# Perceiver stack on one core: the prologue reordered and one context normalised on three engines, and the last chunk's convolution, logarithm and final group rewritten

## The chip, the cores and the metric

The kernel runs on 1 core of one Trainium2 chip, as one launch. The metric is the device time of that launch in microseconds, the median of three runs. The engines are TensorE (PE, with its weight loads PEld), VectorE (DVE), ScalarE (ACT), GpSimd (POOL), and SyncE (SP), whose queue issues nearly all DMAs.

## The reference, cut to what matters

Sixteen batches of 64 latent rows of 128 features (`x`) attend to 1601 context rows per batch, twice, with a scan and a feed-forward after each attention. All is float32.

```python
x = x + xattn0(ctx, ln(x))         # 16 heads of 64; keys/values: 1601 context rows + 64 latents
x = x + selective_scan(ln(x))      # layer 0 "attn"
x = x + moe(ln(x))                 # layer 0 "ffn", 8 experts, top 2
x = x + xattn1(ctx, ln(x), mask)   # layer 1, masked
x = x + ssd(ln(x))                 # layer 1 "attn"
x = x + fp4_ffn(ln(x))             # layer 1 "ffn", blockwise FP4 quantised

# ssd, per batch of 64 tokens, 256 inner channels, 4 heads:
x, z = split(h @ in_proj.T)
x = silu(conv1d_causal(x, conv_w, width=4) + conv_b)
dt = softplus(x @ dt_w.T + dt_b)   # 4 values per token
h  = exp(A * dt) * h + dt * B * x ; y = C . h + D * x
out = (ln(y) * silu(z)) @ out_proj.T
```

## The kernel before

**Staging.** Attention is cut into 64 groups, each a layer, a batch and half of the heads. A group has `NT = 13` steps: step i takes 128 keys against 512 columns (8 heads by 64 latents). The global step number is n, from 0 to 832 for the scores. `step(n)` issues the scores of tile n, and the weighted average (`average`) of the tile `LAG = 21` steps behind. Scores land in PSUM (tag `s`, 3 buffers), ACT copies them to SBUF (`st`, line 625 with mask, 627 without), DVE keeps a running maximum (`R`, lines 632 and 634). `maximum`, `spread` and `weigh` turn them into exponentials (DVE line 669, ACT line 670), and `average` adds 13 products into one PSUM tile `av` (line 682), of which there is one buffer. `gather` (line 693) reads it, `denominator` divides, `turn` transposes, `output` multiplies by the folded output weights `wvo` and adds to the residual `X`. For the last group a few extra matmuls without use (`fill`) are placed on PE in the waits.

**What runs between.** `run` holds two lists. `prep` holds generators that prepare contexts, queries and latents, each with the step n from which it may run; each live one is advanced by one `yield` per step, and a yielded tuple such as `HOP3 = (3,)` makes it sit out three steps. `between` holds the scans and feed-forwards, advanced within a budget per step (0.65 to 1.0 a step, capped at 2.0), in which a yielded number is the cost that is charged. `behind` keeps what it encloses from being issued ahead of the attention instructions of its step, and a scheduler then fixes each engine's static order. In layer 1 the last stages are `scan1` and `ffn` for chunk 6 and chunk 7 (128 tokens each). Chunk 6 may run from n = 810, chunk 7 only when the last group's result is in `X`: it is the tail after the attention. After n = 853 what is left of all stages is issued interleaved.

**Prologue.** `setup` issues the first loads and warms PE with 12 `fill` matmuls. It then advances the generators `latents`, `fold_qk`, `queries` and `first_context` in an order written out by hand, and `in_order` freezes that order for each engine. `first_context` normalises batch 0's context in blocks of four tiles: statistics on DVE (`bn_stats`), the power −1/2 on POOL, the scaling on DVE, ACT or POOL. `context` does it for every later batch: the mean by two DVE reductions (line 571), the variance by 13 ACT squares with an accumulated sum (line 577), the power on POOL (line 129), POOL's offset (line 583), 13 ACT scalings (line 586), a store to DRAM, PE transposes (line 594) and ACT copies into `kvT` (line 595). Scores of batch 1 begin at n = 26. `with_latents` scales `kv` on POOL (line 556). The loads of context 2 (`context_load`) are issued at n = 8.

**The tail.** `scan1` for one chunk: layer norm (`moments`: DVE statistics, POOL multiply-add, POOL power), transpose to `hT`, projection `xz` (line 1055), ACT copy to the padded `xp`, the convolution as 8 DVE operations (lines 1066 and 1068), tanh (1071), then `dt` with a softplus (abs, exp, add, ACT `Ln` at line 1107, corrections), decays `af` (1119, 1151, 1154), `gm` (1161), `sy` (1167), layer norm, gate, `project`. `ffn`: layer norm, `quant` (line 1205 on), two projections (1262, 1263), silu, `quant` of 22 blocks, four transposes (1277), one ACT copy (1279), eight matmul records (1285), the addition and the store. PSUM tiles of these stages come from `tp`, 3 buffers.

Of the kernel before, what the change touches and what calls it, by code (L numbers as in the profile page):

```python
# [70 lines left out]

CG = 2
# [5 lines left out]
class Kernel:  # L78
# [35 lines left out]

    def fill(self, n, after=None):


        t = self.pss.tile([P, NQ], F32, tag="s", name="fill")
        free = mybir.DependencyInfo(mybir.DependencyClass.NoSync, mybir.DependencyReason.DATA)
        for _ in range(n):  # L120
            if after is None:
                mm = self.nc.tensor.matmul(t[:, :P], self.ident, self.ident, start=True, stop=True)
            else:
                mm = self.nc.tensor.matmul(t[:, :2 * P], self.ident, self.wvo[:, :2, :].rearrange("p h d -> p (h d)"), start=True, stop=True)
                self.tc.add_manual_dep(mm.ins, after.ins.name, free, reason="fill")
# [5 lines left out]
    def moments(self, src, n, outs, square=False):  # L131
# [14 lines left out]
        for a, b in outs:  # L146
            v, r = self.sm([P, n], f"var{n}"), self.sm([P, n], f"rstd{n}", bufs=4)
            nc.gpsimd.tensor_scalar(v, var, a, b, ALU.mult, ALU.add)
            self.rsqrt(r, v, n)
            rs.append(r)  # L150
# [6 lines left out]
    def layernorm(self, dst, src, n):  # L157

        mv, (r,) = self.moments(src, n, [LN])
# [5 lines left out]
    def transpose_tokens(self, dst, src, n, name, w=None, b=None):  # L165
# [5 lines left out]
        if w is None:  # L171
            nc.scalar.copy(dst, t[:, :n * P])
# [30 lines left out]
    def setup(self):  # L203
# [3 lines left out]
        self.fill(12)  # L207
# [4 lines left out]
        nc.sync.dma_start(out=self.X[:, :CG], in_=xs[:, :CG])  # L212
        self.raw0 = [self.raw_pair(0, "WqT", "WkT", 0, nc.scalar)]
        rows = self.at.tile([12, D], F32, tag="vrow", name="vrow")
        nc.scalar.dma_start(out=rows, in_=a["vec128"].rearrange("(n d) -> n d", d=D))
# [21 lines left out]
        nc.vector.tensor_scalar_mul(self.nvcol, t[:, :12], -1.0)  # L237

        for g in (context, fold, fold, latents, latents, context, context, queries, queries, context, queries):
            next(g)  # L240
        self.in_order()
# [238 lines left out]
    def first_context(self):  # L480
# [6 lines left out]
        mv = self.sm([P, n, 2], "fmv", bufs=1)  # L487
# [21 lines left out]
        def turned(lo, hi):  # L509
# [4 lines left out]
            nc.scalar.activation(kvT[:, lo * P:lo * P + w], t[:, :w], AF.Copy, scale=self.vcol[:, w1:w1 + 1])  # L514
# [7 lines left out]
        yield 0.0  # L522
# [39 lines left out]
    def context(self, lay, b):  # L562
# [5 lines left out]
        if lay == 0:  # L568
# [16 lines left out]
            for k in range(n):  # L585
                nc.scalar.activation(kv[:, k, :D], kv[:, k, :D], AF.Identity, scale=rstd[:, k:k + 1], bias=off[:, k:k + 1])  # L586
                if k % 5 == 4:
                    yield 0.0
            nc.sync.dma_start(out=self.xh[b], in_=kv[:, :, :D])
# [82 lines left out]
    def average(self, g, i):  # L672
# [6 lines left out]
        for k in range(4):  # L679
            o = grp["av"][:, k // 2, k % 2 * (D + 1):(k % 2 + 1) * (D + 1)]  # L680
            st = grp["st"][i // 2][:, i % 2, k * P:(k + 1) * P]
            mm = nc.tensor.matmul(o, st, self.kv_of[lay, b][0][:, i, :], start=(i == 0 and k % 2 == 0), stop=(i == NT - 1 and k % 2 == 1))  # L682
        if (g, i) == (len(self.groups) - 1, NT - 1):
            self.fill(3, mm)
# [11 lines left out]

    def denominator(self, g):
# [3 lines left out]

        eng = nc.vector if g == len(self.groups) - 1 else nc.gpsimd
        eng.tensor_tensor(aq[:, :, :D], aq[:, :, :D], self.bc(rd, [P, 4, D]), ALU.mult)  # L703
# [327 lines left out]

    def scan1(self, c0, CG):
# [5 lines left out]
        with tc.tile_pool(name="sd1", bufs=1) as one, tc.tile_pool(name="sd2", bufs=CG) as work:  # L1038
# [6 lines left out]
            xi, hT = t1([P, CG, D], "xi"), t1([P, TG], "hT")  # L1045
            xp = t1([P, 2, BG, L + 3], "xp")
            nc.gpsimd.memset(xp, 0.0)
            yield from self.layernorm(xi, X, CG)
# [4 lines left out]
            t = self.tp("xz")  # L1053
            for k in range(2):
                mm = nc.tensor.matmul(t[:, k * TG:(k + 1) * TG], inT[:, k * P:(k + 1) * P], hT, start=True, stop=True)
            if last:
                self.fill(9, mm)
            nc.scalar.copy(xp[:, :, :, 3:], t[:, :2 * TG].rearrange("p (k b l) -> p k b l", k=2, l=L))
            yield 0.5
            yield HOP1  # L1060

            cv = self.tp("cv")
            for k in range(2):
                o = cv[:, k * TG:(k + 1) * TG].rearrange("p (b l) -> p b l", l=L)
                cw = lambda i: self.half[:, 4 * k + i:4 * k + i + 1]
                nc.vector.tensor_scalar(o, xp[:, k, :, 0:L], cw(0), self.half[:, 8 + k:9 + k], ALU.mult, ALU.add)
                for i in range(1, 4):
                    nc.vector.scalar_tensor_tensor(o, xp[:, k, :, i:i + L], cw(i), o, ALU.mult, ALU.add)
                yield 1.6
# [12 lines left out]
            e, w, ln = (t1(shape, n) for n in ("spe", "spw", "spl"))  # L1082
# [12 lines left out]
            nc.vector.tensor_scalar_add(w, e, 1.0)  # L1095
            nc.vector.scalar_tensor_tensor(fl(z), fl(zb), 1.0, t[:, :2 * TG], ALU.add, ALU.mult)
            yield 0.8
# [9 lines left out]
            nc.scalar.activation(ln, w, AF.Ln)  # L1107
            nc.vector.scalar_tensor_tensor(w, w, 1.0, e, ALU.subtract, ALU.subtract)
# [3 lines left out]
            nc.vector.tensor_tensor(ln, ln, w, ALU.subtract)  # L1112
            nc.vector.scalar_tensor_tensor(dt, dt, 0.0, ln, ALU.max, ALU.add)
            nc.vector.tensor_tensor(adt, dt, self.row(self.na1, shape), ALU.mult)

            full = [P, NH, P]
            af = [work.tile(full, F32, tag="af", name=f"af{c}") for c in range(CG)]
            for c in range(CG):
                nc.vector.tensor_tensor(af[c], self.row(self.after, full), self.bc(adt[:, c, :], full), ALU.mult)
# [28 lines left out]
            for c in range(CG):  # L1148
                sg = self.tp(f"seg{c}")
                for h in range(NH):  # L1150
                    mm = nc.tensor.matmul(sg[:, h * P:(h + 1) * P], af[c][:, h, :], self.upto, start=True, stop=True)
                if last:
                    self.fill(2, mm)
                nc.scalar.activation(af[c].rearrange("p h t -> p (h t)"), sg, AF.Exp)
                yield 0.1
            for dst, i in ((zb, 2), (z, 0)):
                for k in range(2):
                    nc.scalar.activation(dst[:, k, :], z[:, k, :], AF.Copy, scale=self.ycol[:, i + k:i + k + 1])
            yield HOP1
            for c in range(CG):  # L1160
                nc.vector.tensor_tensor(gm[c], gm[c], af[c], ALU.mult)
# [10 lines left out]
            yield from self.layernorm(y, y, CG)  # L1172
# [18 lines left out]
    def quant(self, dst, src, n, pool, tag, parts=P):  # L1191
# [27 lines left out]
        nc.vector.scalar_tensor_tensor(o3, t, 2.0 ** 22, self.bc(sc, shape), ALU.mult, ALU.mult)  # L1219
# [26 lines left out]
    def ffn(self, c0, CG):  # L1246
# [3 lines left out]
        with tc.tile_pool(name="ff1", bufs=1) as one, tc.tile_pool(name="ff2", bufs=CG) as work:  # L1250
            t1 = lambda shape, name: one.tile(shape, F32, tag=name, name="ff_" + name)
            xi, xT = t1([P, CG, D], "xi"), t1([P, TG], "xT")
            yield from self.layernorm(xi, X, CG)
# [17 lines left out]
            yield from self.quant(flat, flat, CG * I4 // 16, one, "qh")  # L1271
            yield HOP
            hT = []
            for k in range(CG):
                t = self.tp(f"ft{c0}{k}")
                for i in range(4):
                    nc.tensor.transpose(t[:IC, i * P:(i + 1) * P], hb[:, k, i * IC:(i + 1) * IC], self.ident)  # L1277
                hT.append(work.tile([IC, 512], F32, tag="hT", name=f"fh{c0}{k}"))
                nc.scalar.copy(hT[k], t[:IC, :])  # L1279
# [11 lines left out]
    def run(self, out):  # L1291
# [19 lines left out]
        for lay in range(2):  # L1311
# [14 lines left out]
            for b in range(NB):  # L1326
                if lay or b:
                    prep.append((max(start(lay, b) - (28 if lay == 0 else 12), 4), 2 if lay == 0 else 1, self.context(lay, b)))
# [4 lines left out]
        while n < (ng + 1) * NT + LAG + 8 or between:  # L1333
            for lay in range(2):
                for b in range(NB):
                    if (lay or b > 1) and n == max(start(lay, b) - 48, 8):
                        self.context_load(lay, b)
# [85 lines left out]
    def step(self, n, ng):  # L1423
# [5 lines left out]
        if 0 <= ga < ng and ia:  # L1429
# [3 lines left out]
            if ia == NT - 1:  # L1433
                self.gather(ga)
# [15 lines left out]
        if 0 <= d < ng:  # L1450
            lay, b, half = self.groups[d]["key"]
            last = d == ng - 1
            with self.behind():
                if o == 0:
                    self.denominator(d)
                elif o == (1 if last else 4):
                    self.turn(d)
                if last:
                    if o == 1:
                        self.output(lay, b // 2, 1)  # L1460
                elif o == 7 and b % 2 and half:
# [60 lines left out]
```

## Time and profile before

| What | Value |
|---|---|
| three runs | 2028.36, 2030.52, 2031.50 us (median 2030.52) |
| profiled execution | 2023.57 us, its span 2021.8 us |
| PE / DVE / ACT / POOL busy | 98% / 77% / 69% / 26% of the span |
| mean granted TensorE clock | 0.998 |
| first scores on PE | 13.76 us from the start |
| last `average` matmul ends | 1975.99 us |
| result store issued | 2019.23 us |

The views give times in microseconds from the span's start. A timeline line reads: start, duration, engine, source line, operation, output<-inputs, shapes, count, and in brackets the idle time of that engine just before and what ended it. One float32 matmul shows as two records.

### The profile page before, as it was taken

Reading aid. Unit: us, or ns where it says so; the run is one execution under the profiler, and the core shown is the slowest. Engines: PE = TensorE matmul, PEld = TensorE weight load, DVE = VectorE, ACT = ScalarE, POOL = GpSimd, SP = SyncE. Lnnn points to the kernel's source line nnn. Section 1 sums busy time; section 2 is a strip of 40 time slices with the busy share of each in tenths; the row PEclk is TensorE's granted clock in tenths of the full one; section 3 lists DMA queues with packets and bytes.
Section 4 is the critical chain, followed back from the end, with each engine's and each line's share of the span. In section 5 each row is a group of like instructions: output and inputs, shape, how many; then the busy total and the mean of one; then the engine's idle time right before and its main releaser. Section 6 shows DMA issues by size and latency. Waiting matters only on the chain. (4 is left out here: it accounts for less than half of the span.)

```text
span 2021.8 us, 32874 instructions
## 1 busy us (share of the span) xinstructions
PE 1972.1 (98%) x12117; PEld 1497.7 (74%) x12117; DVE 1556.7 (77%) x2898; ACT 1403.0 (69%) x2667; POOL 515.9 (26%) x576
## 2 busy tenths in 40 slices
PE   8999999999999999999999999999999999999997
PEld 5677777676777777778777787777778777787786
DVE  6887667887868887775988777898686978778774
ACT  6887878887768877666767557776566656665651
POOL 4112122543113452121543203542110121101000
PEclk9999999999999999999999999999999999999999
DMA  6221112322022231221221102221110111101000
GB/s 157 68 66 36 52 52 77 84 61 60 27 87 84 60 79 51 65 77 44 67 80 51 38 23 71 75 59 51 44 53 18 57 36 37 44 13 36 23 1 21
DMA packets 141805, 110.54 MB, mean 55 GB/s; under 512 B 11458, under 2 KB 127950, under 8 KB 141646
## 3 DMA queue, kind: packets, MB, share of 16 engines
q1 hardware_dynamic: 141078, 108.19, 18.4%
q8 instruction: 96, 1.57, 0.3%
q14 instruction: 63, 0.52, 0.1%
q10 hardware_dynamic: 568, 0.27, 0.0%
HBM read 79.97 MB, written 27.41 MB: 53 GB/s over the span
## 5 line engine op out<-in xcount | busy, mean ns | idle before, releaser
L682 PEld LDWEIGHTS av<-kv,st 128*128 128x128 f32 x6656 | 850.1, 192 | 315.0 <-issue 286.3
L682 PE MATMUL av<-kv,st 128*128 128x129 f32 x6656 | 866.9, 276 | 8.3 <-ACT st L670 3.9
L620 PE MATMUL s<-qT,kvT 128*128 128x512 f32 x1664 | 850.1, 601 | 15.7 <-DVE R L634 12.4
L669 DVE TENSOR_TENSOR st<-st,mb 128x1024 f32<-128x1024 f32 (+1 forms) x448 | 501.0, 1131 | 1.7 <-PE mb L661 1.5
L670 ACT ACTIVATE st<-st 128x1024 f32<-128x1024 f32 (+1 forms) x448 | 444.6, 996 | 63.1 <-DVE st L669 59.9
L625 ACT ACTIVATE st<-s,mcol 128x512 f32<-128x512 f32 x416 | 283.8, 685 | 223.4 <-PE s L620 178.3
L627 ACT COPY st<-s 128x512 f32<-128x512 f32 x416 | 240.6, 581 | 126.8 <-PE s L620 100.2
L620 PEld LDWEIGHTS s<-qT,kvT 128*128 128x128 f32 x1664 | 258.8, 191 | 84.0 <-DVE R L634 33.6
L632 DVE SCALAR_TENSOR_TENSOR R<-s,mcol,R 128x512 f32<-128x512 f32 x352 | 261.6, 743 | 70.7 <-ACT st L625 69.5
L634 DVE TENSOR_TENSOR R<-s,R 128x512 f32<-128x512 f32 x352 | 240.6, 684 | 84.2 <-ACT st L627 82.7
L556 POOL TENSOR_TENSOR kv<-kv,vec 128x384 f32<-128x384 f32 (+1 forms) x128 | 136.2, 1084 | 150.4 <-PE kt L594 65.2
L703 POOL TENSOR_TENSOR aq<-aq,rd 128x512 f32<-128x512 f32 x63 | 77.0, 1222 | 356.1 <-DVE rd L700 346.5
L807 POOL TENSOR_TENSOR db<-sc_u,bb 128x512 f32<-128x512 f32 x64 | 85.2, 1334 | 136.0 <-DVE h L818 62.2
L824 POOL TENSOR_TENSOR sc_y<-sc_y,h 128x512 f32<-128x512 f32 x60 | 79.9, 1332 | 103.9 <-DVE h L823 79.9
L586 ACT ACTIVATE kv<-kv,coff,crstd 128x128 f32<-128x128 f32 x195 | 81.6, 490 | 7.5 <-POOL coff L583 7.5
L818 DVE TENSOR_TENSOR_SCAN h<-da,db 128x512 f32<-128x512 f32 x64 | 85.9, 1342 | 0.0
L577 ACT ACTIVATE scr<-kv,cmean 128x128 f32<-128x128 f32 x195 | 78.1, 401 | 6.5 <-DVE cmean L573 3.1
L634 DVE TENSOR_TENSOR R<-s,st 128x512 f32<-128x512 f32 x32 | 22.1, 689 | 72.7 <-ACT st L627 72.7
L693 DVE SCALAR_TENSOR_TENSOR aq<-xeb,ee,av 128x129 f32<-128x129 f32 x256 | 73.7, 339 | 3.4 <-PE av L682 3.4
L129 POOL TENSOR_TENSOR crstd<-cvar,neghalf 128x13 f32<-128x13 f32 x15 | 37.5, 2498 | 141.0 <-DVE cvar L581 140.8
L442 PE MATMUL q<-xnT,wqk 128*128 128x128 f32 x512 | 68.7, 277 | 0.8 <-ACT xnT L176 0.7
L442 PEld LDWEIGHTS q<-xnT,wqk 128*128 128x128 f32 x512 | 62.9, 192 | 6.9 <-issue 2.9
(377 smaller groups left out, 1964.5 us busy)
## 6 DMA issues: line engine op xcount, KB each, us to landing
bb<-bcd SPq DMA_DIRECT2D x64, 256.0 KB, 4.5
xh<-kv SPq DMA_DIRECT2D x16, 832.0 KB, 4.7
kv<-xh SPq DMA_DIRECT2D x16, 832.0 KB, 5.3
kvT<-xhT SPq DMA_DIRECT2D x16, 800.0 KB, 4.6
xhT<-kvT SPq DMA_DIRECT2D x15, 800.0 KB, 3.5
kv<-in_ctx_dram SPq DMA_DIRECT2D x15, 768.0 KB, 5.4
ew<-in_e1T_dram SPq DMA_DIRECT2D x36, 64.0 KB, 1.8
ew<-in_e3T_dram SPq DMA_DIRECT2D x36, 64.0 KB, 1.9
```

Of the source, the lines that this page charges most:

```text
L442: nc.tensor.matmul(t[:, k * P:(k + 1) * P], self.wqk[:, g * 4 + k, :], xnT, start=True, stop=True)
L556: nc.gpsimd.tensor_tensor(kv[:, lo:hi, :D], kv[:, lo:hi, :D], self.row(self.vec[:, w1, :], [P, hi - lo, D]), ALU.mult)
L620: mm = nc.tensor.matmul(s, self.kv_of[lay, b][1][:, i * P:(i + 1) * P], q, start=True, stop=True)
L625: ev = nc.scalar.activation(st, s, AF.Identity, bias=mc)
L627: ev = nc.scalar.copy(st, s)
L632: mx = nc.vector.scalar_tensor_tensor(R, s, mc, last, ALU.add, ALU.max)
L634: mx = nc.vector.tensor_tensor(R, s, last, ALU.max)
L669: nc.vector.tensor_tensor(st, st, self.row(mb, [P, n, NQ]), ALU.subtract)
L670: nc.scalar.activation(st, st, AF.Exp)
L682: mm = nc.tensor.matmul(o, st, self.kv_of[lay, b][0][:, i, :], start=(i == 0 and k % 2 == 0), stop=(i == NT - 1 and k % 2 == 1))
L807: nc.gpsimd.tensor_tensor(db, u, self.row(bb[:, 0, s % 2, :], both), ALU.mult)
L818: nc.vector.tensor_tensor_scan(flat(h), flat(da), flat(db), 0.0, ALU.mult, ALU.add)
```

## The change

It touches three places, and the order of some work around them.

- **Prologue.** The small vector load `vrow` moves from ACT's queue to SP's, ahead of the weights. One warm-up matmul fewer. The generators advance in another order: the latents' scaling before the context statistics, and the latents' transposes between the two weight folds; `nvcol` is computed after them. The evacuation of the first four transposed tiles is split into 128 and 384 columns. `context(0, 1)` starts at n = 3 in place of 4 and takes its statistics by `bn_stats` on DVE, and scales 8 tiles on ACT and 5 on POOL. `context_load` in the loop is put behind the hand-ordered prologue.
- **Chunks 6 and 7.** While chunk 6 runs, `shifted_weights` multiplies the convolution taps into `inT`. In chunk 7 the convolution is then ten matmuls into one PSUM tile (two of them the bias), reading the padded `hT` at four offsets. In all five calls of `scan1` the ACT logarithm becomes a series on DVE. In chunk 7 only, the decays run in two halves, the silu of the gate is placed after `af`, its scalings after the exponential, and the layer norms do the multiply-add on DVE. In the last `ffn` the final quantiser operation, the transposes and the copies run in two halves.
- **Last group.** `finish` replaces `gather`, `denominator`, `turn` and `output`: it works by blocks of 128 columns on DVE, ACT and PE, and the 3 fill matmuls after the last `average` go.

```diff
@@ setup
-        self.fill(12)
+        self.fill(11)
...
+        rows = self.at.tile([12, D], F32, tag="vrow", name="vrow")
+        nc.sync.dma_start(out=rows, in_=a["vec128"].rearrange("(n d) -> n d", d=D))
         self.raw0 = [self.raw_pair(0, "WqT", "WkT", 0, nc.scalar)]
-        rows = self.at.tile([12, D], F32, tag="vrow", name="vrow")
-        nc.scalar.dma_start(out=rows, in_=a["vec128"].rearrange("(n d) -> n d", d=D))
...
-        nc.vector.tensor_scalar_mul(self.nvcol, t[:, :12], -1.0)
-        for g in (context, fold, fold, latents, latents, context, context, queries, queries, context, queries):
+        for g in (latents, context, fold, latents, fold, context, queries, queries, context, queries):
             next(g)
+        nc.vector.tensor_scalar_mul(self.nvcol, self.vcol, -1.0)
@@ context
+        if (lay, b) == (0, 1):
...
+            for k in range(n):
+                bs = self.sm([P, 6], "fbs")
+                nc.vector.bn_stats(bs, kv[:, k, :D])
+                nc.vector.bn_aggr(mv[:, k, :], bs)
+                if k % 2:
+                    yield 1.0
+            nc.vector.tensor_scalar_add(rstd, mv[:, :, 1], EPS)
+            self.rsqrt(rstd, rstd, n)
+            nc.gpsimd.tensor_tensor(off, mv[:, :, 0], rstd, ALU.mult)
+            nc.gpsimd.tensor_scalar(off, off, -1.0, None, ALU.mult)
+            for k in range(8, n):
+                nc.gpsimd.tensor_scalar(kv[:, k, :D], kv[:, k, :D], mv[:, k, 0:1], rstd[:, k:k + 1], ALU.subtract, ALU.mult)
+            yield HOP3
+            for k in range(8):
+                nc.scalar.activation(kv[:, k, :D], kv[:, k, :D], AF.Identity, scale=rstd[:, k:k + 1], bias=off[:, k:k + 1])
+                if k % 2:
+                    yield 1.0
@@ finish (new, last group only)
+        nc.vector.tensor_tensor(four(den), blocks[:, :, :, D], four(grp["ee"]), ALU.add)
+        nc.vector.reciprocal(rd, den)
+        for k in range(4):
+            nc.vector.scalar_tensor_tensor(aq[:, k, :D], xeb[:, :D], grp["ee"][:, k:k + 1], blocks[:, k // 2, k % 2, :D], ALU.mult, ALU.add)
+        for k in range(4):
+            nc.scalar.activation(aq[:, k, :D], aq[:, k, :D], AF.Copy, scale=rd[:, k:k + 1])
+            at = self.pss.tile([P, NQ], F32, tag="s", name=f"at{g}_{k}") if k < 3 else self.tp(f"at{g}_{k}")
+            nc.tensor.transpose(at[:, :P], aq[:, k, :D], self.ident)
+        for k in range(4):
...
+            if k < 2:
+                nc.vector.tensor_scalar(to, at, self.vcol[:, b1:b1 + 1], None, ALU.add)
+            else:
+                nc.scalar.activation(to, at, AF.Identity, bias=self.vcol[:, b1:b1 + 1])
+        self.output(lay, b // 2, 1)
@@ shifted_weights (new, called in chunk 6)
+        for k in range(2):
+            t = self.spread(self.half[:, 4 * k:4 * k + 4], f"cw{k}").rearrange("p (i n) -> p i n", i=4)
+            w = raw(4, f"wcv{k}")
+            nc.vector.tensor_tensor(w, t, self.row(inT[:, k * P:(k + 1) * P], [P, 4, P]), ALU.mult)
+        t = self.tp("cb")
+        for k in range(2):
+            nc.tensor.transpose(t[:1, k * P:(k + 1) * P], self.half[:, 8 + k:9 + k], self.ident)
+        nc.vector.tensor_copy(self.wcb, t[:1, :2 * P])
@@ scan1
+            if last:
+                for k in range(2):
+                    nc.tensor.matmul(o, self.wcb[:, k * P:(k + 1) * P], self.one, start=(k == 0), stop=False)
+                for k in range(2):
+                    for i in range(4):
+                        mm = nc.tensor.matmul(o, self.wcv[k][:, i, :], padded[:, :, i:i + L], start=False, stop=(k == 1 and i == 3))
+                self.fill(3, mm)
...
+            nc.vector.tensor_scalar_add(w, e, 2.0)
+            nc.vector.reciprocal(w, w)
+            nc.vector.scalar_tensor_tensor(v, e, 2.0, w, ALU.mult, ALU.mult)
+            nc.vector.scalar_tensor_tensor(w, v, 0.25, v, ALU.mult, ALU.mult)
+            nc.vector.tensor_scalar(ln, w, ARTANH[4], None, ALU.mult)
+            for i in (3, 2, 1):
+                nc.vector.scalar_tensor_tensor(ln, ln, ARTANH[i], w, ALU.add, ALU.mult)
+            nc.vector.scalar_tensor_tensor(ln, ln, ARTANH[0], v, ALU.add, ALU.mult)
...
-            nc.scalar.activation(ln, w, AF.Ln)
-            nc.vector.scalar_tensor_tensor(w, w, 1.0, e, ALU.subtract, ALU.subtract)
-            nc.vector.tensor_tensor(ln, ln, w, ALU.subtract)
...
+            parts = ((0, 2), (2, NH)) if last else ((0, NH),)
@@ run
-                    prep.append((max(start(lay, b) - (28 if lay == 0 else 12), 4), 2 if lay == 0 else 1, self.context(lay, b)))
+                    prep.append((max(start(lay, b) - (28 if lay == 0 else 12), 3), 2 if lay == 0 else 1, self.context(lay, b)))
...
-                        self.context_load(lay, b)
+                        with self.behind():
+                            self.context_load(lay, b)
```

## The prediction

> **What bounds the kernel now.** I read the page's header first, then busy time by windows, then the timelines of the first 66 and last 90 us. The page says that PE is the bound:
>
> ```profile
> PE 1972.1 (98%) x12117; PEld 1497.7 (74%) x12117; DVE 1556.7 (77%) x2898; ACT 1403.0 (69%) x2667; POOL 515.9 (26%) x576
> ```
>
> A score step without other work repeats every 1.75 us on PE (1934.82 to 1936.57 in the timeline). In windows of 20 us from 60 to 1980, PE is busy 1888.8 of 1920 us: the middle holds 31 us of idle time in all, spread over thirty windows. So little can be won or lost there except by PE work itself. The ends are different. Busy time by windows (PE, PEld, DVE, ACT, POOL, granted clock, DMA share, GB/s) shows one hole in the prologue:
>
> ```profile
> 49.00:53.00 4.00, 0.83 (x5) 0.45 (x4) 2.47 (x4) 4.00 (x9) 0.00 (x0) 1.00 0.10 31
> 53.00:57.10 4.10, 4.10 (x17) 2.95 (x18) 4.09 (x6) 3.48 (x7) 0.51 (x1) 0.58 0.58 181
> ```
>
> PE idles 3.17 us while ACT is full, and then runs for 4.1 us at clock 0.58. The timeline names the cause:
>
> ```profile
> 43.30 2.46 POOL L129 TENSOR_TENSOR crstd<-cvar,neghalf 128x13 f32<-128x13 f32 x1 [8.15 <-DVE cvar L581]
> ...
> 46.09 2.42 ACT L586 ACTIVATE kv<-kv,coff,crstd 128x128 f32<-128x128 f32 x6 [2.43 <-POOL coff L583]
> ...
> 52.86 1.32 PE L682 MATMUL av<-kv,st 128*128 128x129 f32 x8 [3.11 <-ACT st L670]
> ```
>
> ACT first waits 2.43 us for POOL's offsets, then scales 13 tiles in a bunch. The copies and exponentials behind them on ACT come late, and PE starves. The third place is after the last `average` (1975.99): 43 us of a chain in which only one engine works at a time. Its lines for the steps that change:
>
> ```profile
> 1976.03 1.13 DVE L693 SCALAR_TENSOR_TENSOR aq<-xeb,ee,av 128x129 f32<-128x129 f32 x4 [3.16 <-PE av L682]
> ...
> 1981.73 0.29 DVE L730 TENSOR_TENSOR X<-X,o 128x128 f32<-128x128 f32 x1 [3.23 <-PE o L726]
> ...
> 1986.38 1.14 DVE L1068 SCALAR_TENSOR_TENSOR cv<-sd_xp,half,cv 128x128 f32<-128x128 f32 x3
> ...
> 1989.18 0.38 ACT L1071 ACTIVATE sd_th<-cv 128x256 f32<-128x256 f32 x1 [3.28 <-DVE cv L1068]
> ...
> 1991.67 1.28 ACT L1107 ACT_TABLE_LOAD   x1
> ...
> 1995.16 1.28 ACT L1154 ACT_TABLE_LOAD   x1
> ```
>
> The brackets (idle before, and who ended it) show a hand-over at each line: what shortens a link here shortens the run.
>
> **What the Trainium skill says.** "ScalarE: Activation LUTs", section "What ACT_TABLE_LOAD costs", gives about 1283 ns for the load plus about 1380 ns of drain. The trace agrees on the load (1.28 us); `Ln` starts 0.01 us after it ends, so the drain isn't seen here. Its section on table sets puts exp and tanh in one set, and no load stands between them here. "TensorE: Matmul & The Clock Gate", Part 1, says that an idle window of about 3.4 us halves PE's clock; the 3.17 us hole followed by 0.58 agrees. "SBUF — State Buffer", section "Who interferes with whom", says that a DVE operation with two SBUF inputs contends with POOL's reads: line 1131 on POOL takes 1.10 us at 1994.05 beside such an operation (`af`) and 0.62 us at 1928.13 without one. I take it as agreeing.
>
> **The change part by part.**
>
> *Start of the prologue.* Now the first score waits until 13.76: `nvcol` and the context statistics hold DVE, so the latents' scaling runs at 8.79 although its rstd is ready at 5.53; the transposes follow at 9.19, `xnT` at 9.88, queries from 10.49, kt transposes at 12.38, the 512-column copy at 13.02. In the new order scaling runs at 5.6 to 6.2, statistics 6.2 to 7.9, the power to 9.2, block scaling to 10.4. On PE: one fold 6.4 to 7.4, latents' transposes to 7.8, the second fold to 8.7, queries 8.7 to 10.6, kt transposes to 11.2. A 128-column copy (0.3 us) ends at 11.55. So the first score stands at about 11.6: **-2.1 us**. `vrow` on SP delays the context loads by its 0.43 us of issue; statistics first needed at 6.2 hide that. If the weights land later than 6.4 (they were first used at 6.60, and nothing shows how early they were there), the gain shrinks: 0.5 to 2.6.
>
> *Context 1.* Removed from ACT: 13 squares with their accumulator reads (13 x 0.60 = 7.8 us) and 5 scalings (2.0). Added to DVE: 13 x (0.26 + 0.17) = 5.6, less two reductions (2.0) and one small one. Added to POOL: 5 x 0.80 = 4.0. What goes is the hole: 3.17 plus 4.1 x 0.42 = 1.7 lost to the clock, **-4.9**. What comes: DVE in 20 to 33 us was busy about 9 us and gets 3.4 more; its maxima (0.68 a step), which free the score buffers, queue behind the statistics. POOL's 2.46 us power remains, and if `with_latents` of batch 0 (3.87, same step n = 9) stands ahead of it, the ACT scalings at n = 12, and the copies behind them, wait; three score buffers and other PE work cover some 3 us. I take +0.9 for both: **-4.0**, between +1 and -5.5. The load of context 2 moved out of the prologue's SP queue (it held SP at 11.26 to 16.65 together with the rest): nothing on the path, since that context is used at n = 24.
>
> *Middle.* `shifted_weights` adds PE work where PE is the bound: two spreads of 0.60 (as `mb`, line 661) and two transposes, **+1.5**. Its DVE work (2 x 0.69 and a copy) falls in a window where DVE is busy 18 of 20. The series has 9 small DVE operations for 3, +1 us per call in four calls beside PE. Eight table loads (10.3 us of ACT) go there; PE's idle time around them is at most 1 us. The charged budget rises by 1.3 per call, so chunk 6's `ffn` ends about a step (1.75 us) later; `w_inT` at 1978.32 waits for its last matmuls, but the new convolution doesn't use that load. Together **+1.2**, from -1 to +4, most of it for a schedule that shifts.
>
> *Last group.* Now `av` end to the addition takes 5.74. New: two small DVE operations (0.4), first block 0.29, four ACT scalings at 0.41 (the pitch of line 586) to 2.4, last transpose and two ACT evacuations to 3.2, the last two heads' four records and drain 0.55, or all eight heads after the last transpose, to 4.55. I take 4.4: **-1.3** (-0.8 to -2.0). The three fills that go leave PE free for chunk 6's `fo`.
>
> *Convolution.* From `hT` (1984.67) to tanh (1989.18) 4.51. New: 16 records of 128 columns, which line 726 does in 2.05; the four bias records run while ACT copies `hT`. **-2.4** (-1.9 to -2.6).
>
> *Softplus, decays.* From the add at 1991.38 to `adt`'s end 2.57; new 11 dependent operations at the row's pitch of 0.20: 2.2, **-0.4**. From `af`'s end to `sy` added 4.43; the second load overlaps `seg` but delays the exponential by 0.5; halves overlap seg, exp and gm: about 2.75. `sz`'s PSUM tile now stays held until the silu after `af`, with two of three `tp` buffers left for what follows, so I take **-1.5** (-0.7 to -2.0). The silu (0.42) itself lies beside `seg`.
>
> *Layer norms.* One POOL hop of 0.09 saved, three times: **-0.3**. *Last quantiser.* 0.53 becomes two of about 0.34 (352 columns 0.53, 128 columns 0.29), but ft, copy and fo of the first half run beside the second: from 3.05 to 2.2, **-0.8** (-0.4 to -1.0).
>
> Tail: 1.3 + 2.4 + 0.4 + 1.5 + 0.3 + 0.8 = 6.7. Sum: -2.1 - 4.0 + 1.2 - 6.7 = **-11.6** against the profiled execution's 2023.57, which is 7 us under the median of the runs shown; the parts are stalls and fixed operations, so I subtract the same from the median: 2030.5 - 11.6 = 2018.9, said as 2019.
>
> **The rivals.**
> - *The hole only moves.* POOL's power and `with_latents` hold the ACT scalings, so nothing of the -4.9 comes back. For: ACT waits 2.43 on POOL already. Against: ACT has 9.8 us less to do, and the scalings come in pairs, a step apart. Sum -7.6 with the +1.2 kept: 2023.
> - *The tail's chain is mostly kept.* `sz`'s buffer blocks `sx` behind the silu, chunk 6's late `ffn` (DVE operations of 0.53) sits in `finish`'s gaps, the halves give nothing: tail -3.5, prologue -3.5, middle +3: 2026.5.
> - *Slower.* POOL becomes the bound of the prologue: `with_latents`, power, offsets and five scalings in a row are 3.87 + 2.46 + 0.44 + 4.0 = 10.8; if ACT's in-order queue waits for the end of it, beyond the 3 us of cover, PE idles 7.8 and then runs at half clock for some 4 us (2 lost). It costs 9.8 against the hole's 4.9; to outweigh tail and start (8.8) it needs a second such gap, at the first `average` (n = 21) when `kv` isn't scaled yet. Decision point: PE gaps over 13 us in the first 65. About 2036.
> - *The parts don't run as drawn.* The convolution's matmuls at unaligned offsets or a cold PE could take twice 2.05; that alone is 2 us.
>
> **How the numbers follow.** About 0.2% (4 us) is what a measurement of this kernel can tell from no change. Forecast 55%; the moved hole 22%, still faster; the kept tail 13%, which straddles that bound; slower 4%; the rest more gain than drawn (both ends of the unknown costs at their best, -17). Faster 0.88, same 0.08, slower 0.04. Range 2013 to 2026: the low end is the sum of the best bounds, the high end takes in the moved hole and half of the kept tail.
>
> **What would show it.** First score at 11.6 instead of 13.76; no PE idle of 3 us and no clock under 0.9 between 45 and 60; no ACT_TABLE_LOAD at `scan1`; last `average` about 5 us earlier; from its end to the store 36.6 us where it is 43.24 now; tanh 2.1 us after `hT`. Wrong would be: an ACT wait on `off` over 4 us, `af` to `sy` over 4 us, or a last `average` that is not earlier at all.

## The result and the profile after

The changed kernel takes 2021.95 us, median of six runs (2018.29 to 2025.95), against 2030.43 for six of the kernel before: ratio 0.9962, 95% interval 0.9944 to 0.9979, **8.5 us faster**. In a second set of twelve runs it took 2023.15 (0.9961, 0.9946 to 0.9976). The profiled execution took 2023.47, its span 2021.7. PE does as much as before (1972.1 us busy then), as its row of the page's busy times says:

```profile
PE 1974.8 (98%) x12123; PEld 1499.8 (74%) x12123; DVE 1563.8 (77%) x2954; ACT 1382.3 (68%) x2628; POOL 520.5 (26%) x579
```

Busy time by windows of the changed kernel (PE, PEld, DVE, ACT, POOL, granted clock, DMA share, GB/s). The last two rows are the ones that held the hole and the clock of 0.58. PE is all but full in both now, at clock 1.00. The first row shows what is left: PE idle 0.69 of 3 us. POOL is full beside it, but by the timeline below (at 37.33) this wait ends with a DMA of weights.

```profile
35.00:38.00 3.00, 2.31 (x10) 1.08 (x9) 0.00 (x0) 1.14 (x3) 2.92 (x6) 1.00 0.64 190
...
49.00:53.00 4.00, 3.88 (x23) 2.97 (x23) 4.00 (x13) 3.86 (x9) 2.23 (x3) 1.00 0.28 79
53.00:57.10 4.10, 4.10 (x22) 2.55 (x20) 3.07 (x6) 2.54 (x5) 0.00 (x0) 1.00 0.51 200
```

Its timeline in the prologue. The first fold waits for the weights' DMA, so the first score stands at 12.11 (13.76 before; forecast 11.6). ACT's wait for the offsets is still there, 3.20 us, but nine microseconds earlier, and no hole of PE follows it.

```profile
6.64 1.13 PE L341 MATMUL WqT<-rawWqT 64*128 64x128 f32 x8 [0.82 <-DMA rawWqT<-in_L0WkT_dram]
...
12.11 1.12 PE L651 MATMUL s<-qT,kvT 128*128 128x512 f32 x2 [0.46 <-ACT kvT L524]
...
33.04 2.46 POOL L135 TENSOR_TENSOR crstd<-crstd,neghalf 128x13 f32<-128x13 f32 x1
...
36.86 0.88 ACT L595 ACTIVATE kv<-kv,coff,crstd 128x128 f32<-128x128 f32 x2 [3.20 <-POOL coff L590]
...
37.33 1.13 PE L341 MATMUL WvT<-rawWvT 64*128 64x128 f32 x8 [0.69 <-DMA rawWvT<-in_L0Wo_dram]
```

And in the tail, after the last `average` at 1980.92:

```profile
1981.38 0.83 DVE L741 SCALAR_TENSOR_TENSOR aq<-xeb,ee,av 128x128 f32<-128x128 f32 x3
...
1984.98 0.29 DVE L789 TENSOR_TENSOR X<-X,o 128x128 f32<-128x128 f32 x1 [1.96 <-PE o L785]
...
1987.60 0.29 DVE L1400 TENSOR_TENSOR X<-X,fo 128x128 f32<-128x128 f32 x1 [1.60 <-PE fo L1399]
1987.81 0.34 DVE L162 TENSOR_SCALAR sd_xi<-X,mv,rstd 128x128 f32<-128x128 f32 x1
...
1989.16 2.05 PE L1148 MATMUL cv<-sd_hp,wcv 128*128 128x128 f32 x16
...
1991.25 0.38 ACT L1166 ACTIVATE sd_th<-cv 128x256 f32<-128x256 f32 x1 [2.30 <-PE cv L1148]
...
1996.84 1.16 PE L1258 MATMUL seg<-upto,af 128*128 128x128 f32 x8 [0.20 <-DVE sd_z L1225]
```

The tanh starts 2.29 us after `hT` (4.51 before), and neither ACT_TABLE_LOAD is there. But the scaling of `sd_xi` waits for an addition of chunk 6 (`fo`, line 1400), and `seg` waits for the silu. From the last `average` to the store it is 38.21 us where it was 43.24.

**Positions.** Each engine's order is fixed, so how far a kernel leads or trails can be read at the start of each group's transposes `mb`. The table gives that start less the one of the kernel before (us, from the timelines; less than zero is a lead), the end of the last `average` likewise, and the tail from there to the end of the last `X` addition. Columns 0 to 63 are groups.

The granted clock disturbs this. Windows of 2 us find stretches in which it is 0.50. Each lasts 3.4 us and so costs a PE that is busy 1.7, or a multiple where several follow each other. They are called half-clock stretches below. The column "apart" is the one before it with 1.7 taken off for each stretch up to there, and with the two stretches of the kernel before (at 53 and 394) counted likewise.

| Kernel | 0 | 3 | 48 | 61 | 63 | last average | apart | tail |
|---|---|---|---|---|---|---|---|---|
| before | 0 | 0 | 0 | 0 | 0 | 0 | 0 | 43.21 |
| changed | -1.30 | -5.94 | 1.33 | 4.88 | 5.69 | 4.93 | -0.19 | 38.19 |
| changed, again | -1.06 | -5.70 | 0.56 | 4.26 | 5.07 | 4.31 | -0.81 | 38.20 |
| prologue alone | -1.47 | -6.12 | -1.08 | -1.14 | -1.13 | 0.19 | -4.93 | 43.21 |
| order alone | 2.20 | -2.97 | 2.72 | 2.72 | 2.72 | 2.73 | -2.39 | 43.23 |
| norms alone | 0.11 | -0.44 | 3.08 | 3.07 | 3.08 | 3.08 | -2.05 | 43.21 |
| changed, old norms | 4.71 | -0.90 | -0.36 | 1.81 | 2.62 | 1.86 | 0.15 | 38.18 |
| series alone | -0.17 | -0.14 | 6.10 | 9.81 | 9.52 | 8.75 | 1.92 | 43.21 |
| tail alone, `Ln` | 3.26 | 3.27 | 3.13 | 3.10 | 5.18 | 6.40 | 1.28 | 38.77 |
| changed, `Ln` before the last | -1.65 | -6.30 | -2.81 | -2.83 | -0.75 | 0.57 | -1.14 | 38.16 |
| four edits | -1.02 | -5.84 | -2.31 | -0.41 | -0.70 | -1.46 | -3.17 | 36.87 |
| four edits, again | -1.84 | -7.07 | 0.11 | 3.87 | 3.58 | 2.81 | -2.31 | 36.88 |
| four edits, `Ln` | 1.69 | -3.88 | -0.53 | -0.53 | 0.34 | -1.33 | -3.04 | 37.86 |
| four edits, old charge | -1.59 | -6.88 | 2.16 | 1.93 | 1.64 | 0.88 | -5.95 | 36.87 |

The changed kernel leads by 5.94 at group 3 and trails by 1.33 at group 48. Half-clock stretches are a large part of that. The changed kernel's profile has five between groups 3 and 61 (482, 758, two from 830, 1718), that of the kernel before one (394): the four more are 6.8 of the 10.9 us between -5.94 and +4.93. The kernel before's 2023.57 was a profile with few of them; its mean clock was 0.998, in 131 further runs 0.994 on average.

For whole runs there are two rough measures of the same. The loss to the clock is the span times one less the mean clock; the full-clock time is the span times the mean clock. The 131 runs of the kernel before lose 11.4 us on average, the 18 of the changed kernel 8.3; the median full-clock time falls from 2017.6 to 2012.7. Both also count half clock that comes after the last store was issued and costs nothing (1 us in the profile of the kernel before).

### The profile page after: what moved, and what is told of

Same layout as the page of the kernel before. It is cut to its first block, busy times and chain, and to the rows that moved or that the text cites. A ratio compares the mean times of both kernels' runs of the same rounds, so it can differ in the third digit from the quotient of the medians.

```text
span 2021.7 us, 32901 instructions
## 1 busy us (share of the span) xinstructions
PE 1974.8 (98%) x12123; PEld 1499.8 (74%) x12123; DVE 1563.8 (77%) x2954; ACT 1382.3 (68%) x2628; POOL 520.5 (26%) x579
## 5 line engine op out<-in xcount | busy, mean ns | idle before, releaser
L616 ACT ACTIVATE kv<-kv,coff,crstd 128x128 f32<-128x128 f32 x182 | 76.5, 489 | 5.1 <-POOL coff L613 5.1
L607 ACT ACTIVATE scr<-kv,cmean 128x128 f32<-128x128 f32 x182 | 72.8, 400 | 6.9 <-DVE cmean L603 3.7
```

## The experiments

Ratios are to the kernel before on the same chip, with 95% intervals.

### The prologue alone, the order alone, the norms alone

```diff
 kernel before; "order": setup and first_context, "norms": context(0, 1) and run
-        for g in (context, fold, fold, latents, latents, context, context, queries, queries, context, queries):
+        for g in (latents, context, fold, latents, fold, context, queries, queries, context, queries):
...
+        if (lay, b) == (0, 1):
```

> The kernel before with the prologue's part alone: new order of the setup, second context's norms on three engines, its stages one step earlier, next contexts loaded behind the step. In the two profiles the first groups' maxima stood 5.9 us earlier after the change. Theory A (that lead is kept to the end, and what was lost in the middle came from other parts or from slow-clock episodes): 5 to 7 us faster than before, first score at 12.1, no clock under 0.9 between 40 and 60. Theory B (a lead at the start is eaten up again by waits in the middle that don't depend on it): under 3 us faster, and the lead in the starts of the maxima shrinks between groups 15 and 60 as it did in the changed kernel.

Measured: 2023.80 us, 0.9972 (0.9963 to 0.9982), 6.5 us under the kernel before. It leads by 6.12 at group 3 and loses nothing between groups 48 and 61. Its drop before group 48 is three half-clock stretches in a row from 826 on; with half clock apart the lead is kept to the end (4.93). That is theory A.

> The kernel before with the new order of the setup alone; the second context's norms, its start and the loads stay as before. Theory A (the 6.1 us that the whole prologue part won are two separate things: an earlier start, and the hole at 50 us): first score at 12.1 and the maxima of group 3 at most 1.7 us earlier than before, the hole and the half clock after it still there. Theory B (the order of the setup itself removes the hole, since the statistics come earlier): 4 us or more earlier at group 3, no clock under 0.9 at 50 to 60.

Measured: 2030.62, 1.0001 (0.9989 to 1.0012). First score at 11.75. Group 3 leads by 2.97, more than A allows and less than B: ACT's squares start at 25.79 in place of 29.93, the offsets are there at 42.55 in place of 46.05, and no 3 us hole follows (from the first score to 60 PE's longest wait is 0.78). This profile has a half-clock stretch at 33 to 37. So the order takes about 1 us of the hole beside an earlier start of 2.0. The time shows nothing of that: its runs lose 13.2 us to the clock, those of the kernel before on the same chip 11.4.

> The kernel before with the second context's part alone: norms on DVE, POOL and ACT, started at n = 3, next contexts loaded behind the step; the order of the setup stays as before. The new order alone moved the maxima of group 3 by 2.97 us with a half-clock stretch of 1.7 in that profile, so by some 4.7 without one; both parts together moved them by 6.1. Theory A (the hole at 50 us goes with either part, so the two overlap): group 3 some 3 to 5 us earlier, first score unchanged at 13.8. Theory B (they add up): 1.4 us earlier only, the hole still there. On the loss to the clock (span times one less the mean clock): 11 us if it does nothing there, 8 if it is this part that made the loss smaller in every kernel that has it.

Measured: 2026.73, 0.9984 (0.9973 to 0.9995). Group 3 leads by 0.44 only, less than either theory has it, but with two half-clock stretches, where the kernel before has one. The hole has shrunk (PE idles 0.89 us between 49 and 53, where it was 3.17), and half clock follows it all the same. The loss to the clock is 10.5, near the 11 expected if this part does nothing to it. Windows of this kernel; the clock is the third figure from the right:

```profile
53.00:58.00 5.00, 5.00 (x18) 3.42 (x19) 2.68 (x9) 1.38 (x4) 0.91 (x1) 0.66 0.61 223
63.00:68.00 5.00, 5.00 (x23) 3.62 (x22) 5.00 (x10) 1.66 (x3) 0.00 (x0) 0.66 0.29 75
```

Counted without the clock (1.7 a stretch), order gives 3.0, norms 2.1, both 4.4: they nearly add up, which is nearer to theory B, though the hole isn't as it was. The rest of the 6.1 is the one stretch that both together take away.

```diff
 changed kernel
-        if (lay, b) == (0, 1):
```

> The changed kernel with the second context's part taken back alone (squares on ACT, scalings in a bunch, start at n = 4). Theory A (the order of the setup already took most of the hole): the maxima of group 3 some 1.4 us later than in the changed kernel, half-clock stretches apart. Theory B (without the new norms the hole is back): 4 us or more later. If it is this part that lowers the loss to the clock, that loss is 13 us here where the changed kernel has 8; if not, 8 in both, and the time about 2024.

Measured: 2026.03, 0.9972 (0.9961 to 0.9982). Group 3 leads by 0.90 only, 5 us less than in the changed kernel, and two stretches stand at 38 to 46, in windows of this kernel:

```profile
38.00:42.00 4.00, 2.91 (x13) 2.49 (x14) 1.54 (x5) 0.47 (x3) 2.67 (x2) 0.65 0.65 193
42.00:46.00 4.00, 4.00 (x9) 2.04 (x8) 0.00 (x0) 2.54 (x7) 0.00 (x0) 0.50 0.17 50
```

Less 3.4 for the clock that is 1.6 later than the changed kernel, as A says. The mean loss to the clock is 12.2 us here, near the 13 expected if these norms lower it. Over all sets it is 10.5 to 14.4 in the kernels that lack the order or the norms and 5.7 to 8.8 in those with both; six of six profiles of the first kind have a half-clock stretch in the first 70 us, none of eight of the second. A last part of the gain is thus fewer half-clock stretches, and it takes order and norms together. Why the two keep the clock isn't shown.

### The series, and the tail without it

```diff
 kernel before
-            nc.scalar.activation(ln, w, AF.Ln)
+            for i in (3, 2, 1):
+                nc.vector.scalar_tensor_tensor(ln, ln, ARTANH[i], w, ALU.add, ALU.mult)
```

> The kernel before with the logarithm as a series in all five scan1 calls, nothing else. Theory A (its larger budget pushes the later stages of each chunk and makes the previous chunk's quantiser meet the gather): 1 to 4 us slower than before, with the loss between groups 50 and 63 in the trace, less 0.4 won in the last chunk. Theory B (the loss in the middle was slow-clock episodes by chance): within 1 us of before.

Measured: 2032.86, 1.0014 (1.0000 to 1.0029), slower by 2.5 where the interval allows 0 to 6. The trace shows the place: 3.71 lost between groups 48 and 61, then 1.06 won back up to the last average. One half-clock stretch (1722) is in the 3.71, so 1.9 remain at the last average (column "apart"). Its runs also lose 14.4 us to the clock, against 11.1 before. The tail is 43.21 as before: the 0.4 of the last chunk didn't come, since there the silu stands among the series' operations on DVE.

```diff
 changed kernel
+            if not last:
+                nc.scalar.activation(ln, w, AF.Ln)
```

> The changed kernel with the series in the last chunk only; the four calls before it keep Ln and its pauses. Theory A (the series in the middle costs by its budget): 1 to 4 us faster than the changed kernel, 10 to 12 faster than before, and fo of the chunk before the last off the path between the last X addition and the scaled xi (1.84 us there, not 2.88). Theory B (chance episodes): the same as the changed kernel, 8 to 9 faster than before, with the 2.88 unchanged.

Measured: 2024.06, 0.9966 (0.9952 to 0.9981): as the changed kernel, which is what theory B says of the time. Between groups 48 and 61 it loses 0.02 (3.55 there), so the part of A on the place holds. But the shifted weights then cost 2.08 instead of 0.81 (groups 61 to 63), and a half-clock stretch at 1960 follows. From group 48 to the last average both lose the same (3.38 and 3.60). And the 2.88 stays (2.87): the series isn't what makes `fo` late.

```diff
 kernel before, with finish, shifted_weights, the halves and the late silu
             nc.scalar.activation(ln, w, AF.Ln)
```

> The kernel before with the last chunk's parts alone: last group by blocks, convolution by shifted products, decays and last quantiser by halves, small norms on DVE, late silu; Ln stays as the logarithm in all five calls. Theory A (the parts add up, and the chunk before it does not come later without the series): from the last average to the store 37.5 us or less against 43.24, plus 1.5 us of PE for the shifted weights, so 4 to 5 us faster than before. Theory B (the previous chunk's last products stand in the way with or without the series): 38.5 or more, 3 to 4 us faster.

Measured: 2029.92, 1.0003 (0.9991 to 1.0015). The tail is 38.77 to the last addition, 4.4 less; that is theory B's size. Of this the shifted weights take back 2.08. That leaves 2.4, and even so small a gain lies just outside the interval (down to -1.8): neither theory has the time right. Its runs lost 13.4 to the clock on average against 11.1 before; whether that is chance stays open.

### Four edits, and the old charge

```diff
 changed kernel
+            if c0 + CG == C - 1:     # ffn, after fo's matmuls; step drains up to here ahead of finish
+                self.summed = True
+                yield 0.0
-            t = self.tp("sz")
+            t = self.pss.tile([P, NQ], F32, tag="s", name="sz") if last else self.tp("sz")
+            nc.sync.dma_start(out=self.wcv[k].rearrange("p i n -> p (i n)"), in_=conv[512 * k:512 * (k + 1)].partition_broadcast(P))
-            nc.gpsimd.tensor_tensor(off, mv[:, :, 0], rstd, ALU.mult)
-            nc.gpsimd.tensor_scalar(off, off, -1.0, None, ALU.mult)
+            nc.vector.scalar_tensor_tensor(off, mv[:, :, 0], -1.0, rstd, ALU.mult, ALU.mult)
```

> The changed kernel with four edits: fo of the chunk before the last ahead of the last group's transposes, sz of the last chunk in a buffer of the score pool, the shifted weights from a DMA broadcast of the convolution's weights instead of PE transposes, and the second context's offsets by one DVE operation instead of two POOL ones. Theory A (each stood on the path where the trace put it): X addition to scaled xi 1.84 instead of 2.88; end of adt to end of the y addition 4.2 instead of 4.51; the maxima of groups 61 to 63 lose 0 instead of 0.8; the PE gap at 36 to 38 shorter by 0.7: 3 us less than the changed kernel on the full-clock time. Theory B (PE is full, so what one link gives the next takes): under 1 us less.

> The version with the four edits on the changed kernel once more, for its time beside the others of this call: 2012 to 2018, median 2014 to 2015, span times mean clock 2007.

Measured: 2014.02, 0.9921 (0.9901 to 0.9941), and in a second set 2018.60, 0.9942 (0.9919 to 0.9964), six runs each. The tail of this version (first profile), from its timeline:

```profile
1974.36 1.10 PE L1402 MATMUL fo<-wdT,fh 88*128 88x128 f32 x8
...
1978.59 0.29 DVE L788 TENSOR_TENSOR X<-X,o 128x128 f32<-128x128 f32 x1 [1.76 <-PE o L784]
...
1980.28 0.35 DVE L162 TENSOR_SCALAR sd_xi<-X,mv,rstd 128x128 f32<-128x128 f32 x1 [0.66 <-POOL rstd L135]
```

`fo` runs in the wait right after the last average (1974.53), and from the `X` addition to the scaled `xi` it is 1.75 in place of 2.88. The shifted weights by DMA take 1.10 out of groups 61 to 63 (-0.29 against 0.81). The buffer for `sz` gives 0.12 of an expected 0.3. What the offsets on DVE do can't be told: group 3 leads by 3.88 to 7.07 in the four profiles with that edit, by 5.70 to 6.30 in four without. The PE gap at 36 to 38, which was to shrink, is 1.20 in the first profile and 0.58 in the second, and now ends on DVE. In the changed kernel it had ended on a DMA of weights, not on the offsets.

The links that the trace tells make 2.4 us. The full-clock time is 2006.8 and 2007.6 in the two sets, against 2012.7: 5 to 6 less, where theory A said 3 and theory B under 1. What goes beyond 2.4 is not assigned to an edit. In the first profile 2.0 us of it lie between groups 3 and 48, mostly at a wait (at 757 us of the changed kernel, shown in the part on the prediction) that this version has short in one profile and long in the other. The second set was expected at 2012 to 2018, with a full-clock time of 2007. Its median of 2018.60 lies above that, its full-clock time does not: it loses 8.7 us to the clock on average, where the first set lost 5.7.

> The same four edits on the version that keeps Ln in the four calls before the last. Theory A: 4 us less than that version and the best of all on the full-clock time, about 2008; in its trace the maxima of groups 61 to 63 lose nothing where that version loses 2.1. Theory B: within 1 us of that version.

Measured: 2016.63, 0.9929 (0.9910 to 0.9948), full-clock time 2006.8. That is about 6 less than the version without the edits has (2012.7), near theory A, but no better than the four edits with the series. The groups 61 to 63 still lose 0.87 where nothing was expected. And `fo` isn't ready when the last average ends, and put ahead of the last group it delays it: the `X` addition comes 5.29 after the average in place of 4.35. So the 1.1 us that the later link won (1.74 from the addition to the scaled `xi`), the earlier one lost but for 0.2, and the tail is 37.86 and not 36.87.

```diff
 four edits
-            yield 1.5
+            yield 0.5
...
-                yield 0.6
+                yield 0.3
```

> The version with the four edits, and the series in all calls charged to the budget as Ln was (0.5 and 0.3 in place of 1.5 and 0.6); the operations are the same. Theory A (what the series costs between groups 48 and 61, 1.9 us in the profile of that version and 3.6 where a half-clock stretch follows, comes from the charge, which shifts the stages behind it): that loss is gone, 1 to 3 us faster than the version with the four edits. Theory B (the operations themselves on DVE make it): the loss stays within 0.5 us.

Measured: **2012.25**, 0.9914 (0.9892 to 0.9936), the fastest here: 6.4 under the four edits in the same set of runs, 1.8 under their first set. The intervals overlap; the full-clock time is 2004.5, 3 less than theirs in the same set. Between groups 48 and 61 it gains 0.23, where the four edits lost 1.90 and 3.76. That is theory A: the operations cost nothing there, their charge did. How, the timeline of the changed kernel shows:

```profile
1706.32 0.35 DVE L722 SCALAR_TENSOR_TENSOR aq<-xeb,ee,av 128x129 f32<-128x129 f32 x1
...
1708.58 0.34 DVE L722 SCALAR_TENSOR_TENSOR aq<-xeb,ee,av 128x129 f32<-128x129 f32 x1
...
1711.22 5.19 POOL L565 TENSOR_TENSOR kv<-kv,vec 128x512 f32<-128x512 f32 x4 [5.34 <-DMA kv<-xh]
...
1716.37 1.04 POOL L762 TENSOR_TENSOR aq<-aq,rd 128x512 f32<-128x512 f32 x1
...
1717.46 0.66 PE L773 MATMUL at<-ident,aq 128*128 128x128 f32 x4 [1.97 <-POOL aq L762]
```

The quantiser of the `ffn` of chunks 2 and 3, later by the charge, falls between the four records of `gather`, and the next `average` starts later. Its DVE operations then run beside POOL's four `kv` operations, which take 5.19 us. The division on POOL stands behind these, and PE idles 1.97 us for it. With the old charge, in that kernel's timeline, `gather` is in one piece, the four take 4.05, and PE waits 0.40:

```profile
1707.45 1.12 DVE L721 SCALAR_TENSOR_TENSOR aq<-xeb,ee,av 128x129 f32<-128x129 f32 x4
...
1711.73 4.05 POOL L565 TENSOR_TENSOR kv<-kv,vec 128x512 f32<-128x512 f32 x4 [5.66 <-DMA kv<-xh]
...
1716.83 0.66 PE L772 MATMUL at<-ident,aq 128*128 128x128 f32 x4 [0.40 <-POOL aq L761]
```

The profiles split cleanly. In the six with the larger charge POOL's four operations take 5.17 to 5.19 us and PE waits 1.97 to 2.26; in the other eight they take 4.04 to 4.51, and PE waits 0.39 to 0.42.

### The changed kernel again

> The changed kernel once more, unchanged. If the half-clock stretches of its first profile (482, 758, 830 and 1718 us) belong to the kernel, they come again at the same places; if they are drawn anew in each execution, only those that follow an idle PE come again, and some of them are missing. The time is expected at 2018 to 2026, and the product of span and mean clock at 2012.9 as before.

Measured: 2023.15, 0.9961 (0.9946 to 0.9976); the full-clock time is 2012.7, as expected. The stretches at 758, 830 and 1718 came again, that at 482 did not, though PE idles there as before, and one at 389 was new. So the places belong to the kernel and the execution draws among them. The expectation was wrong in one point: the one at 830 follows no idle PE and came again.

## Why the prediction was right, point by point

The time, 2021.95, is 3 us above the forecast of 2019 and inside the range. The way there is not quite the one forecast. Of the sum of -11.6, 1.7 was half clock and 9.9 were stalls and operations. With half clock apart, the two profiles of the changed kernel gain 5.2 and 5.8 (last average and tail). The rest of the 8.5, some 2 to 3 us, is half clock: by the rough measure its runs lose 3.1 us less to it, of which about 1 may cost nothing. So the prologue came about as drawn, the tail at three quarters of it, and the middle cost about three times its 1.2. By parts, of the first profile:

- **Start of the prologue**, -2.1: measured -1.65. The bound that was named, the weights, decided: PE waited 0.82 for them.
- **Context 1**, -4.0: with the start, -6.1 was forecast and -5.9 measured at group 3. The attribution was wrong. The step took the whole hole for the new norms. The order took about 1 us of its 3.2, because it let the old squares start 4 us earlier, and only both parts together keep the clock. The rival "the hole only moves" is refuted by the full windows: PE's idle time from the first score to group 3 falls from 5.15 to 2.82.
- **Middle**, +1.2: from group 3 to the last average the lead falls by 4.1 us with half clock apart, in the second profile by 3.2. This is the term of the sum that was mis-sized most; it lies at the upper end of its bounds (-1 to +4). From group 48 on it is 1.9: 1.9 by the series' charge, 1.1 by the shifted weights, less 1.1 won back. The mechanism was right there (the budget shifts a schedule), the place was not: the loss isn't at chunk 6's end but at the quantiser of chunks 2 and 3. In four of six profiles with that charge a half-clock stretch of 1.7 follows, which was not in the sum. The other 2.2 (1.1 in the second profile) lie before group 48 and were not foreseen. 1.2 of them are at one wait, here in the changed kernel and in the kernel before:

```profile
756.74 1.12 PE L651 MATMUL s<-qT,kvT 128*128 128x512 f32 x2 [2.70 <-DVE R L665]
```

```profile
759.83 1.13 PE L620 MATMUL s<-qT,kvT 128*128 128x512 f32 x2 [0.79 <-DVE R L634]
```

This wait isn't tied to the change. It is long (1.97 to 2.70) in eight of the fourteen profiles and short (0.48 to 0.79) in six, and the four edits have it long in one profile and short in the other. In the eight, ACT has just waited 3.4 to 4.2 us for the store of a transposed context (`xhT<-kvT`), in the six 1.9 to 2.3. Why it comes and goes stays open.

- **Tail**, -6.7: measured -5.0. By links, forecast in brackets: last group -1.68 (-1.3), convolution -2.22 (-2.4), softplus -0.3 (-0.4), decays -1.06 (-1.5), quantiser -0.60 (-0.8), the layer norms of the `y` and of the last `ffn` together -0.2. The step that failed is in the last group: "The three fills that go leave PE free for chunk 6's `fo`". The trace has `fo` behind the output and its fills instead, and its addition ahead of the scaling: +1.04, which the rival of the kept tail had named. Moving `fo` gave 1.13 back, and the tail came to 36.87. Of the decays' missing 0.44, `sz`'s buffer explains 0.12.
- **The last average** was to come 5 us earlier, and "a last `average` that is not earlier at all" was named as a sign of being wrong. That sign appeared: it came 4.93 later in this profile and 4.31 in the second. Half-clock stretches make 6.8 of the 10.9 lost since group 3, the middle's 4.1 the rest. With them apart it is 0.2 and 0.8 earlier. So of what the prologue won, the middle took nearly all but the half clock, and the tail carries the gain that is left.

The forecast was set against the median and not against the profiled execution, and that was needed: the profiled execution alone would have told no gain at all (2023.47 against 2023.57). It drew five stretches in the middle, that of the kernel before one.

## What to carry to other kernels

Where a hidden budget orders the work, a charge is a schedule: change an operation and keep its charge first, then look where its neighbours went. Before a chain is shortened, look at what is queued to run in its gaps, and place it by hand. And compare two profiles by their positions along a static order, with the half-clock stretches counted apart, since one profile can draw several more of them than another.

## What was not expected of the hardware

The clock stretches are many, short and drawn anew. In the changed kernel's runs the time goes with the mean clock, from 2018.29 at 0.998 to 2025.95 at 0.995. The Trainium skill ("TensorE: Matmul & The Clock Gate", Part 1) has a window of about 3.4 us that runs free of the kernel; the stretches agree, at 3.4 us each. A full window of idle time isn't needed: at 481 a stretch follows a wait of 2.49 us, and the hole of the kernel before was 3.17. Nor is that wait enough: all fourteen profiles have it (2.48 or 2.49 us), and in seven a stretch follows. And one stretch comes without a wait. Timeline and windows of the changed kernel:

```profile
481.59 0.60 PE L177 MATMUL mot<-ident,mo_nx 128*128 128x128 f32 x2 [2.49 <-DVE mo_nx L162]
...
827.09 1.15 PE L341 MATMUL WqT<-rawWkT,rawWqT 64*128 64x128 f32 x8
828.17 2.05 PE L988 MATMUL mo<-w_fWoT,mo_oT 32*128 32x128 f32 x16
```

```profile
482.00:486.00 4.00, 4.00 (x16) 3.25 (x16) 3.23 (x5) 2.02 (x3) 0.50 (x1) 0.57 0.76 229
...
826.00:830.00 4.00, 4.00 (x33) 3.65 (x31) 3.79 (x5) 2.65 (x4) 0.00 (x0) 1.00 0.25 74
830.00:838.00 8.00, 8.00 (x24) 4.97 (x23) 3.63 (x11) 1.68 (x3) 2.34 (x7) 0.57 0.19 54
```

PE is busy throughout from 826 to 838, and yet has 0.57 of its clock from 830 on; nine of fourteen profiles show this at that place. Just before stand matmuls over 64 and over 32 partitions, in the five profiles without the stretch too. That the clock is set by how much of the array works is a guess; it wasn't tried.
